# State recurrence of a Perceiver layer: B through PSUM, the product with C and half of the state sum on GpSimd

## The chip, the cores and the metric

The kernel runs on one core of a Trainium2 chip. A core has TensorE (PE in the profile, with its weight loads as PEld), VectorE (DVE), ScalarE (ACT), GpSimd (POOL) and SyncE (SP, which here only issues DMAs), each with its own queue of instructions that it takes in order; they meet through semaphores. SBUF is the working memory of 128 partitions, PSUM the memory that TensorE writes, in eight banks of 2 KB per partition. The metric is device time in microseconds (us), the median of several runs; lower is better. A line such as L893 is a line of the kernel's file.

## The reference

The kernel computes one layer over 512 latent rows of width 512: cross attention (16 heads of 64) to a context of 8192 rows, then a state-space block with its MLP, then a mixture of 16 experts. The part that matters here is the recurrence of the state-space block, over 512 steps, 1024 channels and 16 states per channel:

```python
def step(hstate, t):
    delta_t, B_t, C_t, x_t = t
    dA = jnp.exp(delta_t[..., None] * A)
    dBx = (delta_t * x_t)[..., None] * B_t[:, None, :]
    hstate = dA * hstate + dBx
    y = jnp.einsum('bdn,bn->bd', hstate, C_t)
    return (hstate, y)
```

B_t and C_t have 16 values each, the same for all channels; they come from a projection of the convolved input (`x_dbl`). The result is `y + xin * D`, multiplied by `silu(z)` and projected back.

## The kernel before

The file has two large parts. The first, up to about 1948 us of the profiled span, is the cross attention: its TensorE work is laid out by hand, and the rest of the file is ordered by the framework's scheduler, which fixes the order of each engine's queue when the kernel is built. The second part is the function `tail`, a generator, of which the first pieces (the attention's output projection for the first 256 rows, `prep(0)`, `delta(0, 0)`) run beside the attention's last unit, and the rest behind it.

In `tail` the 512 steps are two halves `s` of H = 256 steps, and the 1024 channels are eight blocks `b` of 128, which lie on the partitions. `prep(s)` normalises, projects, convolves and makes `xd`, whose rows 0 to 31 lead to delta, rows 32 to 47 are B and rows 48 to 63 are C. Both are written to DRAM (`bc_d`) and read back by `load_bc` so that every partition holds the same rows: four tiles of 4 states x 256 steps for B (k = 0) and four for C (k = 1), 512 KB each.

`delta(s, q)` makes, for a pair of blocks q, the tiles `dl` (delta), `du` (delta times the input) and `zs` (silu of z). `scan(s, b)` is the recurrence of one block, in four turns of four states each, 64 turns in all. A turn works so, with the engines in brackets:

- L886 (ScalarE), four times: dA = exp(delta x A) into columns 1 to 256 of a `dA` tile of 257 columns per state. Column 0 of dA is zero.
- L888 (ScalarE), second half only: the carried state into column 0 of the tile `hs`.
- L889 (VectorE): B x du into columns 1 to 256 of `hs`, 128x1024.
- L893 (VectorE): one scan over all 4 x 257 columns, state = dA x state + hs, in place. The zero in column 0 of dA stops one state from running into the next, and column 0 of hs is the start value.
- L895 (ScalarE), first half only: the last column into `carry`.
- L896 (VectorE): hs x C, 128x1024.
- L899 (TensorE): four matmuls with the identity add the four states into the PSUM tile `py`; in fp32 each is two records in the profile.

After four turns L900 adds D x input by one more matmul. There are three `dA` and three `hs` tiles, taken in turn. When both blocks of a pair are done, `gate` (L905 to L907, VectorE and ScalarE) multiplies `py` by `zs` and splits the product in two fp16 parts for the output projection. The pieces of `prep(1)` and, in the second half, of the first half's MLP (`ffn`) are put between the scans by the loop from L1030.

PSUM: `ps_s` (two banks), `ps_o` (one), `ps_x` (two) and `ps_j` (three) are opened for the attention and kept to the end; in `tail`, `py` takes its two buffers from `ps_s`, and accumulators of the MLP and the experts come from `ps_s`, `ps_o` and `ps_x` through `acc`.

Of the kernel before, what the change touches and what calls it, by code (L numbers as in the profile page):

```python
# [8 lines left out]
F16 = mybir.dt.float16  # L9
# [28 lines left out]
def perceiver_layer(ctx: ExitStack, tc: tile.TileContext, a: dict, out: bass.AP):  # L38
# [81 lines left out]
    ps_s = ctx.enter_context(tc.tile_pool(name="ps_s", bufs=2, space=PSUM))  # L120
    ps_o = ctx.enter_context(tc.tile_pool(name="ps_o", bufs=1, space=PSUM))
    ps_x = ctx.enter_context(tc.tile_pool(name="ps_x", bufs=2, space=PSUM))
    ps_j = ctx.enter_context(tc.tile_pool(name="ps_j", bufs=3, space=PSUM))
    L = R(late, "late", 1)
# [461 lines left out]
    for m in range(NSTEP):  # L586
        n = NLAST * NSTEP + m
        if m % 4 == 0:
            load(n // 4 + 1)
        cur = scores(u, m, loads[n // 4], sp)  # L590
        while len(pend) > 1:
            drain()
        pend.append((u, m, cur))
        if m == 0:
            tl = tail(tc, a, out, const, scr, ident, x_sb, mlp_d, oT, y_d, xd_d, (ps_s, ps_o, ps_x, ps_j))
        for _ in range(2):
            if m >= 1 and not ready:
                ready = next(tl)
# [6 lines left out]
    late.close()  # L605
    for _ in tl:
        pass


def tail(tc, a, out, const, scr, ident, x_sb, mlp_d, oT, y_d, xd_d, psums):  # L610
# [5 lines left out]
    ps_s, ps_o, ps_x, ps_j = psums  # L616
    nacc = [0]
# [9 lines left out]
    def acc(i):  # L627
        if i < 2:
            return ps_s.tile([P, DM], F32, name=f"acc{i}", tag="pss")
        nacc[0] += 1  # L630
        if nacc[0] % 3 == 0:
            return ps_o.tile([P, DM], F32, name="acc3", tag="po")
        return ps_x.tile([P, DM], F32, name="acc4", tag="px")
# [99 lines left out]
    nc.gpsimd.memset(carry, 0.0)  # L733
    bc_d = [scr.tile([32, H], F32, name=f"bc_d{s}") for s in range(2)]
# [9 lines left out]
    def prep(s):  # L744
# [86 lines left out]
        nc.scalar.copy(dtx[64:96, s], dtx[0:32, s])  # L831
        BC[s] = {}
        load_bc(s, 0, m1)
        yield

    def load_bc(s, k, pool_):
        bf = bc_d[s].rearrange("(o n) t -> o (n t)", o=1)
        for nq in range(4):
            x = pool_.tile([P, 4, H], F32, name=f"bc{k}{nq}")
            o = (k * 16 + nq * 4) * H  # L840
            nc.sync.dma_start(x.rearrange("p n t -> p (n t)"), bf[:, o : o + 4 * H].to_broadcast((P, 4 * H)))
            BC[s][k, nq] = x
# [33 lines left out]
    def scan(s, b):  # L876
        q, j = b // 2, b % 2
        if j == 0:
            dlu[s, q].append(ps_s.tile([P, 2, H], F32, name="py", tag="pss"))
        dl, du, zs, py = dlu[s, q]  # L880
        for nq in range(4):
            dA, hs = dAs[turn[0] % 3], hss[turn[0] % 3]
            turn[0] += 1
            for n in range(4):
                k = nq * 4 + n
                nc.scalar.activation(dA[:, n, 1:], dl[:, j], AF.Exp, scale=Av[:, b, k : k + 1])  # L886
            if s:
                nc.scalar.copy(hs[:, :, 0], carry[:, b, nq * 4 : nq * 4 + 4])  # L888
            nc.vector.tensor_tensor(  # L889
                hs[:, :, 1:], BC[s][0, nq], du[:, j].unsqueeze(1).to_broadcast((P, 4, H)), ALU.mult  # L890
            )
            hf = hs.rearrange("p n t -> p (n t)")
            nc.vector.tensor_tensor_scan(hf, dA.rearrange("p n t -> p (n t)"), hf, 0.0, ALU.mult, ALU.add)  # L893
            if s == 0:
                nc.scalar.copy(carry[:, b, nq * 4 : nq * 4 + 4], hs[:, :, H])  # L895
            nc.vector.tensor_mul(hs[:, :, 1:], hs[:, :, 1:], BC[s][1, nq])  # L896
            for n in range(4):
                k = nq * 4 + n
                nc.tensor.matmul(py[:, j, :], lhsT=ident, rhs=hs[:, n, 1:], start=k == 0, stop=False)  # L899
        nc.tensor.matmul(py[:, j, :], lhsT=dD[:, b], rhs=xin[s][:, b, :], start=False, stop=True)  # L900
# [113 lines left out]
    load_bc(0, 1, m3)  # L1014
    dAs = [m3.tile([P, 4, H + 1], F32, name=f"dA{i}") for i in range(3)]
    hss = [m3.tile([P, 4, H + 1], F32, name=f"hs{i}") for i in range(3)]
    for t in dAs + hss:
        nc.gpsimd.memset(t[:, :, 0:1], 0.0)
# [11 lines left out]
    for i, (s, q) in enumerate(seq):  # L1030
        scan(s, 2 * q)
        if s == 0:
            next(p1, None)
        if i:
            gate(*seq[i - 1], yTs[-1])
        if (s, q) == (1, 0):
            outproj(0, yTs[-1], h2s[0])
            ml = ffn(0, h2s[0], MLP, [acc(3), acc(3)])
            yTs.append(m3.tile([P, 2, 8, H], F16, name="yT", bufs=2))
        if ml and (s, q) != (1, 0):  # L1040
            next(ml, None)
        if i + 1 < len(seq):
            if (s, q) == (0, 3):
                for _ in p1:
                    pass
                load_bc(1, 1, m3)
            delta(*seq[i + 1])
# [9 lines left out]
    M.close()  # L1057

# [37 lines left out]
    mlp1 = ffn(1, h2s[1], MLP, [acc(0), acc(1)])  # L1096
# [6 lines left out]
    rs0 = ffn(0, xT0, RS, [acc(3), acc(3)])  # L1103
# [119 lines left out]
    def moe_down(k, gT, ws):  # L1223
        py = acc(k % 4)
# [28 lines left out]
    for _ in ffn(1, xT1, RS, [acc(3), acc(3)]):  # L1253
        pass
# [84 lines left out]
```

## Time and profile before

| | us |
|---|---|
| median of 3 runs | 2683.66 (2681.24 to 2689.78) |
| the profiled execution | 2681.84 |
| its span | 2679.8 |
| attention and lead-in, 0 to 1948 us | 1948 |
| recurrence, 1948 to 2302 us | 354 |
| MLP of the second half, experts, 2302 to 2680 us | 378 |
| VectorE busy in the recurrence | 337.4 |
| ScalarE busy there | 223.0 |
| GpSimd busy there | 4.8 |

A row of a group reads: line, engine, operation, output <- inputs, shapes, count | busy us, mean ns of one | idle time of the engine just before these instructions and what ended most of it. A row of the order of time reads: start us, duration us, engine, line, operation, and in brackets the idle time before it. Consecutive instructions of one kind may be merged into a row. Instructions of VectorE overlap by some 0.07 us at their ends, so sums of durations are larger than its busy time.

### The profile page before, as it was taken

To read this page: it belongs to the slowest core of one execution; us is meant where nothing else is said; L and a number is where in the kernel's file an instruction comes from. 1 tells how busy PE (TensorE), PEld (TensorE's weight loads), DVE (VectorE), ACT (ScalarE), POOL (GpSimd) and SP (SyncE) were. 2 spreads that over 40 slices of the span, in tenths; PEclk is the share of its full clock that TensorE was granted. 3 is DMA by queue.
4 is the path that set the end of the run, shared out by engine and by line. 5 is a ranking of instruction groups with operands and counts; after the bars stand their busy time and mean duration, and the time that the engine had idled before them with its cause. 6 is when DMAs were issued, how large, how long until landed. Compare 5 with 4: busy or idle time off the path is not lost. (4 is left out here: it accounts for less than half of the span.)

```text
span 2679.8 us, 62328 instructions
## 1 busy us (share of the span) xinstructions
PE 2429.7 (91%) x25902; PEld 1708.1 (64%) x25902; DVE 2052.3 (77%) x2355; ACT 1954.4 (73%) x3701; POOL 44.7 (2%) x58
## 2 busy tenths in 40 slices
PE   7999999999999999998999998887878777898995
PEld 4454676777666677766777767776756555665442
DVE  6786688777878877777877777886799999643785
ACT  5787787888787888867888887786857566432784
POOL 2000000000000000000000000000000000001001
PEclk8999999999999999989999999999989889999998
DMA  7873899766689966668856646666511222575896
GB/s 271 284 264 128 283 290 272 224 171 184 189 266 270 272 171 187 170 192 259 233 169 186 176 134 151 168 169 182 175 63 32 95 71 79 200 255 198 296 338 222
DMA packets 353715, 531.92 MB, mean 198 GB/s; under 512 B 25106, under 2 KB 218834, under 8 KB 353300
## 3 DMA queue, kind: packets, MB, share of 16 engines
q1 hardware_dynamic: 352148, 523.69, 64.6%
q8 instruction: 205, 3.36, 0.5%
q0 software_dynamic: 1280, 4.20, 0.5%
q14 instruction: 82, 0.67, 0.1%
HBM read 397.68 MB, written 126.94 MB: 196 GB/s over the span
## 5 line engine op out<-in xcount | busy, mean ns | idle before, releaser
L361 DVE TENSOR_TENSOR phl<-p,phl 128x1024 f16<-128x1024 f32 x512 | 625.9, 1223 | 194.1 <-ACT phl L358 156.2
L356 ACT ACTIVATE p<-pss 128x512 f32<-128x512 f32 x1024 | 601.3, 612 | 156.1 <-PE pss L349 132.4
L292 ACT ACTIVATE sf<-psx 128x512 f16<-128x512 f32 x1024 | 556.9, 620 | 83.7 <-PE psx L287 80.7
L348 PE MATMUL pss<-qhh,k 128*128 128x256 f16 x2048 | 485.5, 275 | 39.3 <-ACT phl L358 35.3
L349 PE MATMUL pss<-qlm,kb 128*128 128x256 f16 x2048 | 484.6, 275 | 0.0
L378 PE MATMUL po<-v,phl 128*128 128x65 f16 x4096 | 429.8, 195 | 25.0 <-DVE phl L361 24.8
L376 PE MATMUL po<-v,phl 128*128 128x65 f16 x4096 | 434.7, 193 | 3.2 <-DVE phl L360 1.5
L377 PE MATMUL po<-v,phl 128*128 128x64 f16 x4096 | 434.0, 193 | 0.0
L376 PEld LDWEIGHTS <-phl 128*128 128x128 f16 x4096 | 380.1, 98 | 44.5 <-issue 18.5
L378 PEld LDWEIGHTS <-phl 128*128 128x128 f16 x4096 | 379.3, 97 | 29.9 <-DVE phl L361 28.9
L377 PEld LDWEIGHTS <-phl 128*128 128x128 f16 x4096 | 379.7, 97 | 20.9 <-issue 2.0
L300 DVE TENSOR_TENSOR runm<-runm,sf 128x2048 f16<-128x2048 f16 x240 | 292.4, 1218 | 47.4 <-ACT sf L292 46.7
L358 ACT ACTIVATE phl<-pss 128x512 f16<-128x512 f32 x512 | 311.9, 609 | 0.0
L264 PE MATMUL psv<-wh_v,ctxc 128*128 128x256 f16 x1024 | 282.6, 276 | 0.0
L265 PE MATMUL psv<-wl_v,ctxc 128*128 128x256 f16 x1024 | 281.6, 275 | 0.0
L266 PE MATMUL psv<-wh_v,ctxc 128*128 128x256 f16 x1024 | 281.4, 275 | 0.0
L349 PEld LDWEIGHTS <-kb 128*128 128x128 f16 x2048 | 201.1, 98 | 94.5 <-issue 52.6
L348 PEld LDWEIGHTS <-k 128*128 128x128 f16 x2048 | 201.3, 98 | 62.4 <-issue 16.5
L287 PE MATMUL psx<-khl,qh 64*128 64x512 f16 x1024 | 210.6, 392 | 23.1 <-ACT sf L292 19.5
L360 DVE CAST phl<-p 128x1024 f16<-128x1024 f32 x256 | 176.6, 690 | 50.1 <-ACT p L356 46.3
L899 PE MATMUL py<-hs,ident 128*128 128x256 f32 x512 | 146.4, 442 | 70.8 <-DVE hs L896 70.7
L240 PE MATMUL psk<-ctxc,wh_k 128*128 128x512 f16 x512 | 197.2, 385 | 8.5 <-ACT ctxc L223 8.5
(304 smaller groups left out, 4091.3 us busy)
## 6 DMA issues: line engine op xcount, KB each, us to landing
v<-v_d SPq DMA_DIRECT2D x128, 520.0 KB, 4.7
k<-k_d SPq DMA_DIRECT2D x256, 256.0 KB, 4.6
ctxc<-ctx_d SPq DMA_DIRECT2D x96, 512.0 KB, 6.1
wef<-in_gu_dram SPq DMA_DIRECT2D x72, 512.0 KB, 6.2
v_d<-vs SPq DMA_DIRECT2D x128, 260.0 KB, 3.4
k_d<-khl SPq DMA_DIRECT2D x128, 256.0 KB, 3.0
kb<-k_d SPq DMA_DIRECT2D x128, 256.0 KB, 5.2
wpm<-w_d SPq DMA_DIRECT2D x48, 512.0 KB, 4.6
```

What stands on the lines that cost most here:

```text
L264: nc.tensor.matmul(ps[:, t, :], lhsT=ct[i // 2][:, 0, i % 2, sl], rhs=wh[:, i, :], start=i == 0, stop=False)
L265: nc.tensor.matmul(ps[:, t, :], lhsT=ct[i // 2][:, 0, i % 2, sl], rhs=wl[:, i, :], start=False, stop=False)
L292: nc.scalar.activation(dst, ps, AF.Copy, scale=1.0 / (8.0 * WS))
L300: nc.vector.tensor_tensor(r, r, sf, ALU.max)
L348: nc.tensor.matmul(ps[:, hh], lhsT=k[:, hh, sl], rhs=qhh[:, hh, qs], start=True, stop=False)
L349: nc.tensor.matmul(ps[:, hh], lhsT=b[:, hh, sl], rhs=qlm[:, hh, qs], start=False, stop=True)
L356: nc.scalar.activation(p32[:, i], pss[i], AF.Exp, scale=sc)
L358: nc.scalar.activation(ph[:, i], pss[i], AF.Exp, scale=sc)
L361: nc.vector.tensor_tensor(pl, p32, ph, ALU.subtract)
L376: nc.tensor.matmul(o, lhsT=ph[:, i, hh, qs], rhs=vh1, start=first, stop=False, **kw)
L377: nc.tensor.matmul(o[:, 0:64], lhsT=ph[:, i, hh, qs], rhs=vl, start=False, stop=False, **kw)
L378: nc.tensor.matmul(o, lhsT=pl[:, i, hh, qs], rhs=vh1, start=False, stop=last, **kw)
```

## The change

B no longer comes as broadcast tiles. In `prep`, B times 16 is split into three fp16 parts, and three small DMAs put them into rows 0 to 2 of a tile `bhl` whose other rows are zero. A matmul with a weight tile that holds 1/16 everywhere then adds the three rows and gives every partition the sum, 2 states x 256 steps at a time, in a PSUM tile `pb` of two buffers. VectorE multiplies `pb` by `du` in place in PSUM, and scans with dA from SBUF and `pb` from PSUM into `hs`; a turn has two such halves. The tiles dA and hs have 256 columns per state instead of 257: dA's first column is zero, and in the second half the carried state times its decay (`dc`) is added into the first column of `pb` before the scan. The carry is now copied by VectorE.

The product with C runs on GpSimd. In every second turn GpSimd also adds the turn's last two states to its first two, so that TensorE sums two tiles instead of four there. The `gate` of a pair of blocks is called inside the next pair's first scan, after its first turn's product, because `py` has one buffer now. The attention's PSUM pools are closed before the recurrence; it opens a pool of its own (`py` one bank, `pb` two, accumulators two), and a pool of five accumulators follows behind it. The C tiles are loaded by `load_c`, as those of k = 1 were.

```diff
+    bhl = [m1.tile([P, 16 * H], F16, name=f"bhl{s}") for s in range(2)]
+    for t in bhl:
+        nc.gpsimd.memset(t, 0.0)
+    sixteenth = m1.tile([P, P], F16, name="sixteenth")
+    nc.gpsimd.memset(sixteenth, 1.0 / WS)
...
+        bs = m2.tile([64, 3, H], F16, name="bs", tag="w2k", bufs=5)
+        br = m2.tile([64, H], F32, name="br", tag="w2k", bufs=5)
+        rows = slice(32, 48)
+        nc.scalar.activation(bs[rows, 0], xd[rows], AF.Copy, scale=WS)
+        nc.vector.scalar_tensor_tensor(br[rows], xd[rows], WS, bs[rows, 0], ALU.mult, ALU.subtract)
+        nc.scalar.copy(bs[rows, 1], br[rows])
+        nc.vector.tensor_tensor(bs[rows, 2], br[rows], bs[rows, 1], ALU.subtract)
+        for x in range(3):
+            nc.sync.dma_start(bhl[s][x : x + 1, :].rearrange("o (n t) -> o n t", t=H), bs[rows, x])
         BC[s] = {}
-        load_bc(s, 0, m1)
...
+        if s:
+            dc = m2.tile([P, 16], F32, name="dc", bufs=2)
+            nc.scalar.activation(dc, Av[:, b, :], AF.Exp, scale=dl[:, j, 0:1])
+            nc.vector.tensor_mul(dc, dc, carry[:, b, :])
...
-                nc.scalar.activation(dA[:, n, 1:], dl[:, j], AF.Exp, scale=Av[:, b, k : k + 1])
-            if s:
-                nc.scalar.copy(hs[:, :, 0], carry[:, b, nq * 4 : nq * 4 + 4])
-            nc.vector.tensor_tensor(
-                hs[:, :, 1:], BC[s][0, nq], du[:, j].unsqueeze(1).to_broadcast((P, 4, H)), ALU.mult
-            )
-            hf = hs.rearrange("p n t -> p (n t)")
-            nc.vector.tensor_tensor_scan(hf, dA.rearrange("p n t -> p (n t)"), hf, 0.0, ALU.mult, ALU.add)
+                nc.scalar.activation(dA[:, n, 1:], dl[:, j, 1:], AF.Exp, scale=Av[:, b, k : k + 1])
+            for n2 in range(2):
+                k, ns = nq * 4 + 2 * n2, slice(2 * n2, 2 * n2 + 2)
+                pb = accs[-1].tile([P, 2, H], F32, name="pb", tag="pb", bufs=2)
+                nc.tensor.matmul(
+                    pb.rearrange("p n t -> p (n t)"), lhsT=sixteenth, rhs=bhl[s][:, k * H : (k + 2) * H],
+                    start=True, stop=True,
+                )
+                nc.vector.tensor_tensor(pb, pb, du[:, j].unsqueeze(1).to_broadcast((P, 2, H)), ALU.mult)
+                if s:
+                    nc.vector.tensor_tensor(pb[:, :, 0], pb[:, :, 0], dc[:, k : k + 2], ALU.add)
+                nc.vector.tensor_tensor_scan(
+                    hs[:, ns].rearrange("p n t -> p (n t)"), dA[:, ns].rearrange("p n t -> p (n t)"),
+                    pb.rearrange("p n t -> p (n t)"), 0.0, ALU.mult, ALU.add,
+                )
             if s == 0:
-                nc.scalar.copy(carry[:, b, nq * 4 : nq * 4 + 4], hs[:, :, H])
-            nc.vector.tensor_mul(hs[:, :, 1:], hs[:, :, 1:], BC[s][1, nq])
-            for n in range(4):
-                k = nq * 4 + n
-                nc.tensor.matmul(py[:, j, :], lhsT=ident, rhs=hs[:, n, 1:], start=k == 0, stop=False)
+                nc.vector.tensor_copy(carry[:, b, nq * 4 : nq * 4 + 4], hs[:, :, H - 1])
+            nc.gpsimd.tensor_tensor(hs, hs, BC[s][nq], ALU.mult)
+            two = nq % 2
+            if two:
+                nc.gpsimd.tensor_tensor(hs[:, 0:2], hs[:, 0:2], hs[:, 2:4], ALU.add)
+            if before:
+                before()
+                before = None
+            if j == 0 and nq == 0:
+                dlu[s, q].append(accs[-1].tile([P, 2, H], F32, name="py", tag="py", bufs=1))
+            py = dlu[s, q][3]
+            for n in range(2 if two else 4):
+                nc.tensor.matmul(py[:, j, :], lhsT=ident, rhs=hs[:, n, :], start=nq == 0 and n == 0, stop=False)
...
+    pb_s = ExitStack()
+    accs.append(pb_s.enter_context(tc.tile_pool(name="ps_b", bufs=2, space=PSUM)))
+    load_c(0, m3)
...
-        scan(s, 2 * q)
+        scan(s, 2 * q, (lambda: gate(*seq[i - 1], yTs[-1])) if i else None)
         if s == 0:
             next(p1, None)
-        if i:
-            gate(*seq[i - 1], yTs[-1])
...
     M.close()
+    pb_s.close()
+    accs.append(es.enter_context(tc.tile_pool(name="ps_a", bufs=5, space=PSUM)))
```

## The prediction

> **What bounds the kernel now.** I read three views, in this order: busy time by stretch, the groups of instructions in the stretch that the change touches, and the order of time inside it. The state recurrence (`scan`) runs from 1948 us to 2302 us of the span.
>
> ```profile
> core 0: us, PE busy (x) PEld busy (x) DVE busy (x) ACT busy (x) POOL busy (x), PEclk, DMA share, GB/s
> 0.00:1948.00 1948.00, 1832.86 (x22375) 1311.72 (x22376) 1493.85 (x1755) 1536.86 (x2961) 22.99 (x37) 0.98 0.72 210
> 1948.00:2302.00 354.00, 273.79 (x1413) 206.73 (x1412) 337.41 (x301) 223.04 (x497) 4.78 (x5) 0.91 0.21 67
> ```
>
> In this stretch VectorE (DVE) works 337.4 of 354 us, ScalarE 223, the DMA engines a fifth, GpSimd (POOL) 5. VectorE sets the pace here. The groups of the stretch say with what:
>
> ```profile
> L893 DVE TENSOR_TENSOR_SCAN hs<-dA,hs 128x1028 f32<-128x1028 f32 x64 | 145.1, 2287 | 2.8 <-ACT dA L886 2.4
> L896 DVE TENSOR_TENSOR hs<-hs,bc 128x1024 f32<-128x1024 f32 x64 | 76.7, 1212 | 0.8 <-ACT carry L895 0.8
> L889 DVE TENSOR_TENSOR hs<-bc,du 128x1024 f32<-128x1024 f32 x64 | 76.0, 1213 | 0.9 <-PE py L899 0.7
> L905 DVE TENSOR_TENSOR y<-py,zs 128x512 f32<-128x512 f32 x8 | 5.4, 677 | 2.9 <-PE py L900 2.9
> L864 DVE TENSOR_TENSOR du<-dl,xin 128x512 f32<-128x512 f32 x7 | 4.8, 684 | 0.0
> L899 PE MATMUL py<-hs,ident 128*128 128x256 f32 x512 | 146.4, 442 | 70.8 <-DVE hs L896 70.7
> ```
>
> There are 64 turns (2 halves x 8 blocks x 4 groups of 4 states); each costs VectorE a product with B (L889), a scan (L893) and a product with C (L896). Almost no idle time stands before them. TensorE (PE) waits 70.7 us for L896. The order of time shows the pitch:
>
> ```profile
> 2040.06 1.20 DVE L889 TENSOR_TENSOR hs<-bc,du 128x1024 f32<-128x1024 f32 x1
> 2041.18 1.22 DVE L896 TENSOR_TENSOR hs<-hs,bc 128x1024 f32<-128x1024 f32 x1
> 2042.32 2.29 DVE L893 TENSOR_TENSOR_SCAN hs<-dA,hs 128x1028 f32<-128x1028 f32 x1
> 2042.45 2.00 PE L899 MATMUL py<-hs,ident 128*128 128x256 f32 x8 [0.17 <-DVE hs L896]
> 2044.53 1.20 DVE L889 TENSOR_TENSOR hs<-bc,du 128x1024 f32<-128x1024 f32 x1
> ```
>
> Start to start, the products take 1.12 and 1.14 us, the scan 2.21: a turn is 4.47 us of VectorE, 64 turns 286 us. The other 51 of its 337 us are `delta`, `gate`, the second `prep`, norms and splits. The four sums over states of a turn are eight matmul records in about 1.8 us of issue.
>
> **The change, VectorE's demand.** The product with C leaves VectorE: -1.13 us a turn. The product with B and the scan become two halves of 512. From the rows, one element of a product costs (1.13 - 0.06)/1024 and of a scan (2.21 - 0.07)/1028 us, so halves have a pitch of 0.60 and 1.14 us; a turn becomes 2 x 0.60 + 2 x 1.14 = 3.48 us. That is -0.99 x 64 = -63 us. Added: 32 copies of the carry, 64 additions of two elements, 8 products of 16, small splits: about 106 small instructions; such ones (L920, 0.13 us long) start 0.06 to 0.08 us before the next one, so +7 us. VectorE's demand falls from 337 to 281 us, 4.4 a turn.
>
> [...] The row of L905 reads PSUM and takes 677 ns, L864 reads SBUF alone and takes 684. [...]
>
> **GpSimd's price.** It gets 64 products of 1024 and 32 additions of 512. The nearest row is four additions of 512:
>
> ```profile
> L182 POOL TENSOR_TENSOR x_sb<-x_sb,bo_bc x4: 1441/1732/2250, 24.8 to 29.6; 128x512 f32<-128x512 f32 x4
> 24.83 7.04 POOL L182 TENSOR_TENSOR x_sb<-x_sb,bo_bc 128x512 f32<-128x512 f32 x4 [11.73 <-DMA bo_bc<-in_bo_dram]
> ```
>
> Doubled, a product is 2.9 us by the fastest and 3.6 by the mean. [...] During those four, VectorE ran two-input SBUF work (L224, L80). [...]
>
> **What takes the place of the removed work.** In the built order of the changed kernel, TensorE's queue holds the broadcasts of B for turn t+1 mostly behind the sums of turn t-1, and these wait for GpSimd. So a chain closes over two turns: scan t-1 ends, GpSimd multiplies (and adds, in every second turn), TensorE sums, broadcasts, VectorE does turn t+1. Even: hop 0.05 + 2.32 + 0.05 + sums 1.76 + broadcast and hop 0.45 (a 128x512 matmul is 0.38) + 3.56 = 8.2 us. Odd: 0.05 + 2.32 + 1.24 + 0.05 + 0.88 + 0.45 + 3.56 = 8.55. With the small additions of the second half that is 4.23 a turn, 271 us. On top:
> - Other matmuls (z, FFN, convolution) stand between those sums and the next broadcast: about 67 us counted over all turns by the pitches 0.109 (256 columns) and 0.215 (512 columns), of which one parity's chain sees half, 33, and 36 at the clock of 0.91.
> - In seven turns the broadcast stands behind the sums of the turn right before: about 1.7 us beyond what other VectorE work covers, +12. In ten it stands a turn further ahead: -7.
> - Of VectorE's other 51 us most fits into the waits (the chain leaves about 1.3 us a turn); a quarter I count on the chain, +10.
>
> Sum 322 us for the 64 turns.
>
> **Start and end.** Before, the recurrence starts while TensorE is busy with the projection of the attention output:
>
> ```profile
> 1947.22 3.48 DVE L889 TENSOR_TENSOR hs<-bc,du 128x1024 f32<-128x1024 f32 x3
> 1950.81 2.30 DVE L893 TENSOR_TENSOR_SCAN hs<-dA,hs 128x1028 f32<-128x1028 f32 x1
> 1957.95 0.38 PE L688 MATMUL pwo<-wpm,oT 128*128 128x512 f16 x1
> 1958.16 1.89 PE L899 MATMUL py<-hs,ident 128*128 128x256 f32 x8
> ```
>
> After, the first broadcasts stand behind all 48 matmuls of that projection, so the first product starts at about 1958.7, some 11 us later. At the end GpSimd has memsets and the affine select (4.34 us by its row) ahead of its last product, so the last gate comes about 7.7 us after the last scan instead of 5.4 (2295.0 to 2300.4). 1958.7 + 322 + 7.7 = 2288 against 2300: -12 us.
>
> **At nothing.** ScalarE loses 64 small copies of 0.19 us and gains splits; it isn't full. SP loses eight broadcast loads of B (512 KB, 6.2 us to landing) and gains six small loads that fill the three rows of B; the first three are issued in the last attention unit, with tens of us of cover, the second three before the first half's last block is scanned. Uncovered, a chain of loads would cost about 6 us once. Clearing those rows takes GpSimd 2 x 3.8 us (0.95 per 1024, L710) while it is idle. The later stages keep their instructions; their PSUM pools rotate over five buffers. I allow 3 us either way.
>
> Profiled execution 2681.8 (span 2679.8 and 2 us around it) - 12 = 2670; the median of the runs is 1.8 above that execution, so 2672.
>
> **The rivals.**
> - *VectorE stays the bound* (0.20): its idle moments and the matmuls' coincide, the chain is hidden. 281 us of work + its 17 of idle now = 298, + 10 at the start + 2 at the end against 354: -44, 2640. For it: the chain alone is 4.23 a turn against 4.4. Against: the queues are in order and the broadcasts have two PSUM buffers.
> - *GpSimd is slow* (0.27): at 2.9 and 1.45 us the chain grows by 0.58 or 0.79 per two turns, half of that per turn, +22 us; at the mean row +45. So 2694 to 2717, I take 2700. This is the one on the other side. It decides from 0.2 us more a turn (+12 us), a product of about 2.65 us. For it: the only row. Against: what VectorE ran beside that row.
> - *Nothing measurable* (0.17): start delay, in-order matmuls and PSUM's fixed cost eat the rest: 2682.
>
> **How the numbers follow.** Likeliest case 0.36, 2672, its own range 2655 to 2688. Measurement tells about 0.3% (8 us) from no change. Faster: 0.31 of the likeliest, 0.20, and 0.02 of the third, 0.53. Same: 0.04 of the likeliest and 0.13, 0.17. Slower: 0.27 and the rest, 0.30. The range leaves out the tenth beyond a hidden chain and that beyond the mean row: 2640 to 2704.
>
> **What would show it.** Right: the groups of the halves at 0.68 and 1.21 us with no product with C on VectorE; GpSimd's products near 2.3 us; VectorE idle some 40 us or more in the stage, ended by TensorE's broadcasts; the first half-product near 1958. Wrong: products of GpSimd at 2.9 us or more, or stretched by VectorE; halves over 0.75 or 1.3 us (PSUM's price); VectorE still over 95% busy (then faster than I say); or sums that wait on GpSimd with long rows of other matmuls behind them, on average over 5 us a turn.

## The result, and the profile after

The changed kernel takes 2756.50 us (2744.96 to 2763.28) against 2686.72 us (2681.24 to 2690.23) for the kernel before on the same chip: 1.0257 times as long, with a 95% interval of 1.0213 to 1.0301. I had forecast 2672 us, faster, with 2640 to 2704 as the range. The prediction was wrong, in sign and in size. The profiled execution took 2751.74 us, with a span of 2750.0 us against 2679.8 before. Of these +70.2 us:

| stretch of the span | before, us | after, us | difference | forecast |
|---|---|---|---|---|
| last split of the attention's output starts | 1946.8 | 1959.5 | +12.7 | 0 |
| from there to the first product with B | 0.4 | 10.5 | +10.1 | +11.5 |
| from there to the start of the last gate | 353.2 | 403.5 | +50.3 | -23.5 |
| from there to the end | 379.4 | 376.5 | -2.9 | 0 |

Busy time by stretch, changed kernel (columns: the stretch, its length, busy time and instructions of the engines, granted clock of TensorE, DMA share, GB/s):

```profile
core 0: us, PE busy (x) PEld busy (x) DVE busy (x) ACT busy (x) POOL busy (x), PEclk, DMA share, GB/s
0.00:1970.00 1970.00, 1851.23 (x22420) 1319.66 (x22421) 1500.30 (x1761) 1545.91 (x2979) 30.05 (x37) 0.97 0.70 207
1970.00:2374.00 404.00, 287.95 (x1385) 193.57 (x1385) 319.44 (x470) 217.00 (x426) 194.93 (x101) 0.90 0.17 54
```

No engine is full in the recurrence. VectorE was busy 337.4 of 354 us before; it is busy 319.4 of 404 us now, and idle for 84.6. I had forecast 281 us of work in a stage of about 330 us, so some 49 us of idle time. VectorE has 38 us more work than that, and 36 us more idle time. These two numbers are what has to be explained. (The windows and groups here and below are of one profiled execution of each kernel.)

The groups of that stretch, changed kernel. Three lines are pieces that the change left alone (L869 and L872 in `delta`, L935 in `gate`):

```profile
L916 POOL TENSOR_TENSOR hs<-hs,bc 128x1024 f32<-128x1024 f32 x64 | 151.6, 2369 | 217.2 <-DVE carry L915 99.7 <-DVE hs L910 82.5 <-PE pxz L679 12.4
L910 DVE TENSOR_TENSOR_SCAN hs<-dA,pb 128x512 f32<-128x512 f32 x128 | 150.3, 1206 | 1.0 <-DVE pb L909 0.4
L927 PE MATMUL py<-hs,ident 128*128 128x256 f32 x384 | 118.6, 452 | 92.0 <-POOL hs L919 54.0 <-POOL hs L916 37.8
L907 DVE TENSOR_TENSOR pb<-pb,du 128x512 f32<-128x512 f32 x128 | 84.9, 690 | 43.5 <-PE pb L903 43.4
L919 POOL TENSOR_TENSOR hs<-hs 128x512 f32<-128x512 f32 x32 | 42.7, 1334 | 2.5
L869 DVE SCALAR_TENSOR_TENSOR ex<-u,ex 128x512 f32<-128x512 f32 x7 | 10.5, 1494 | 0.6 <-ACT u L867 0.6
L935 DVE TENSOR_TENSOR yT<-y,yT 128x512 f16<-128x512 f32 x7 | 9.2, 1310 | 0.6 <-ACT yT L934 0.6
L872 DVE TENSOR_TENSOR dl<-rl,lgu 128x512 f32<-128x512 f32 x7 | 8.0, 1148 | 0.0
L642 DVE TENSOR_TENSOR r<-r,nw_a 128x2 f32<-128x2 f32 x1 | 2.2, 2194 | 0.0
```

Read the means first. The halves (L907 at 690 ns, L910 at 1206) and GpSimd (2369 and 1334) are what I had forecast. The same three pieces took 684, 680 and 681 ns before and now take 1494, 1310 and 1148; L642, on two elements per partition, took 0.15 us and now takes 2.19. The same four in the kernel before:

```profile
L859 DVE SCALAR_TENSOR_TENSOR ex<-u,ex 128x512 f32<-128x512 f32 x7 | 4.8, 684 | 2.1 <-ACT u L857 2.0
L907 DVE TENSOR_TENSOR yT<-y,yT 128x512 f16<-128x512 f32 x7 | 4.8, 680 | 0.0
L862 DVE TENSOR_TENSOR dl<-rl,lgu 128x512 f32<-128x512 f32 x7 | 4.8, 681 | 0.1
L645 DVE TENSOR_TENSOR r<-r,nw_a 128x2 f32<-128x2 f32 x1 | 0.1, 146 | 0.0
```

Then the last column of the changed kernel's groups: TensorE's sums wait 92.0 us for GpSimd.

The waits of VectorE in the stretch, changed kernel (who waited <- for whom: us in total, times, the longest):

```profile
DVE pb L907 <- PE pb L903: 43.4, 33, 5.8
DVE g L972 <- PE pu L679: 16.4, 6, 6.1
DVE y L933 <- PE py L928: 9.1, 4, 5.6
DVE xs L780 <- ACT xs L778: 7.3, 2, 3.7
```

The broadcasts end 43.4 us of idle time, as forecast. Another 33 us are ended by other work, most of it TensorE's, for which VectorE waited far less before: the MLP's `pu` (it is called FFN in the file), the last sum ahead of a gate, a split of `prep`.

The order of time says when this happens. In a stretch with no long turn the turns start 3.62, 3.88 and 4.43 us apart (over all 64 turns the scans of one turn end 6.26 us behind those of the turn before on average, 5.54 in the median):

```profile
2256.12 1.27 DVE L907 TENSOR_TENSOR pb<-pb,du 128x512 f32<-128x512 f32 x2
2259.74 1.27 DVE L907 TENSOR_TENSOR pb<-pb,du 128x512 f32<-128x512 f32 x2
2263.62 1.35 DVE L907 TENSOR_TENSOR pb<-pb,du 128x512 f32<-128x512 f32 x2 [0.17 <-PE pb L903]
2268.05 0.70 DVE L907 TENSOR_TENSOR pb<-pb,du 128x512 f32<-128x512 f32 x1 [0.65 <-PE pb L903]
```

But seven times more than 10 us lie between the end of one turn's scans and the end of the next turn's; these seven stretches take 93 us and hold 47.7 us of VectorE's idle time. One of them:

```profile
2093.75 2.35 POOL L916 TENSOR_TENSOR hs<-hs,bc 128x1024 f32<-128x1024 f32 x1 [2.78 <-DVE carry L915]
2096.18 1.26 POOL L919 TENSOR_TENSOR hs<-hs 128x512 f32<-128x512 f32 x1
...
2097.49 2.08 PE L927 MATMUL py<-hs,ident 128*128 128x256 f32 x4 [2.32 <-POOL hs L919]
2099.36 1.06 PE L928 MATMUL py<-xin,dD 128*128 128x256 f32 x2
2100.22 0.63 PE L860 MATMUL pd<-dtx,dtw 128*128 128x256 f16 x2
...
2103.27 0.27 PE L679 MATMUL pz<-hT,wpm 128*128 128x256 f16 x1
2103.38 0.59 PE L903 MATMUL pb<-bhl,sixteenth 128*128 128x512 f16 x2
2103.80 1.30 DVE L907 TENSOR_TENSOR pb<-pb,du 128x512 f32<-128x512 f32 x2 [5.81 <-PE pb L903]
```

TensorE waits for GpSimd's addition, does its sums, then the next block's delta and 24 matmuls of z (2100.64 to 2103.38), and only then the broadcast that VectorE has been waiting for.

### The profile page after: what moved, and what is told of

Same layout as the page of the kernel before. It is cut to its first block, busy times and chain, and to the rows that moved or that the text cites. A ratio compares the mean times of both kernels' runs of the same rounds, so it can differ in the third digit from the quotient of the medians.

```text
span 2750.0 us, 62689 instructions
## 1 busy us (share of the span) xinstructions
PE 2461.3 (90%) x25902; PEld 1701.9 (62%) x25902; DVE 2039.2 (74%) x2527; ACT 1957.2 (71%) x3649; POOL 241.2 (9%) x154
## 5 line engine op out<-in xcount | busy, mean ns | idle before, releaser
L927 PE MATMUL py<-hs,ident 128*128 128x256 f32 x384 | 118.6, 452 | 92.0 <-POOL hs L919 54.0
```

## The experiments

Two explanations were set against each other. *Queue* (Q in some of the expectations): the sums over states wait for GpSimd in TensorE's queue, and everything behind them waits too, so where a row stands in that queue decides. *Contention* (L): GpSimd and VectorE hold each other up at SBUF, wherever anything stands. A third, P, put the loss on the broadcasts through two PSUM buffers alone; the first three runs below lie under its limits of 2720, 2720 and 2735 us. Where no other kernel is named, a diff is against the changed kernel. A ratio is to the kernel before on the same chip, whose median there was 2686.7 to 2689.7 us, so that medians of different rows can be compared to about 3 us. All the runs, with the stretch from the first product with B to the last gate's end as "stage":

| kernel | median us | ratio to before (95%) | stage | VectorE busy in it |
|---|---|---|---|---|
| before | 2686.72 | | 353.9 | 338.2 |
| changed | 2756.50 | 1.0257 (1.0213 to 1.0301) | 404.2 | 319.6 |
| no product with C | 2689.83 | 1.0014 (0.9997 to 1.0030) | 344.1 | 289.3 |
| sums read another tile | 2681.19 | 0.9977 (0.9960 to 0.9994) | 332.0 | 315.1 |
| product with C on VectorE | 2715.91 | 1.0113 (1.0051 to 1.0174) | 372.3 | 355.5 |
| before, product with C on GpSimd | 2756.50 | 1.0264 (1.0198 to 1.0330) | 417.7 | 364.2 |
| sums one turn later | 2739.30 | 1.0195 (1.0162 to 1.0227) | 386.2 | 317.2 |
| sums two turns later | 2716.39 | 1.0096 (1.0065 to 1.0126) | 364.2 | 318.2 |
| projection moved | 2749.13 | 1.0224 (1.0196 to 1.0252) | 408.2 | 314.1 |
| no addition on GpSimd | 2758.02 | 1.0246 (1.0213 to 1.0279) | 404.4 | 309.0 |
| two turns + projection | 2705.20 | 1.0066 (1.0044 to 1.0087) | 369.1 | 319.4 |
| ... + fourth buffer | 2707.39 | 1.0062 (1.0040 to 1.0084) | 367.8 | 312.9 |
| ... + three turns | 2693.62 | 1.0021 (1.0012 to 1.0031) | 355.0 | 320.5 |
| ... + sources in PSUM | 2687.35 | 0.9999 (0.9987 to 1.0011) | 347.2 | 309.0 |
| changed, no clearing | 2751.41 | 1.0238 (1.0220 to 1.0256) | 408.5 | 319.3 |
| sources in PSUM, no clearing | 2693.04 | 1.0016 (1.0001 to 1.0030) | 354.9 | 307.7 |
| sources in PSUM, clearing on VectorE | 2675.42 | 0.9946 (0.9930 to 0.9962) | 344.4 | 309.2 |

### The parts of the change, one by one

No product with C, and no addition on GpSimd:

```diff
-            nc.gpsimd.tensor_tensor(hs, hs, BC[s][nq], ALU.mult)
-            two = nq % 2
-            if two:
-                nc.gpsimd.tensor_tensor(hs[:, 0:2], hs[:, 0:2], hs[:, 2:4], ALU.add)
+            two = 0
```

> The changed kernel without the product with C and without the addition of states on GpSimd: TensorE sums the raw states, four per turn (the product with C is left out of the computation). Theory Q (the latency of GpSimd sits in a chain through TensorE's in-order queue to the next broadcast): the chain is gone, VectorE is the bound with about 281 us of work, some 10 us of start delay stay: 2645 to 2670 us. Rival P (the broadcasts of B through two PSUM buffers and TensorE's order are what costs): stays above 2720.

Measured: 2689.83 us, between the two ranges on record. Neither text had seen what TensorE does without GpSimd's addition:

```profile
1962.40:2306.50 344.10, 299.78 (x1526) 199.46 (x1527) 289.32 (x470) 220.45 (x429) 0.73 (x5) 0.98 0.20 64
```

VectorE is busy 289.3 us, 8 more than the 281 of the forecast and 30.3 less than in the changed kernel, although its instructions are the same. TensorE, which sums four tiles in every turn here, is busy 299.8 of 344.1, and VectorE still idles 54.8 us:

```profile
PE py L924 <- DVE hs L910: 38.1, 59, 2.7
DVE pb L907 <- PE pb L903: 36.8, 35, 2.5
```

The sums now wait for the scan, and broadcasts still stand behind them. So even with GpSimd idle, this arrangement with four sums in every turn is no faster than the kernel before (2689.83 us; the profiled execution, 2682.08, is the fastest of its ten), and GpSimd's latency alone doesn't account for the 84.6 us of idle time in the changed kernel.

The sums read dA instead of the products, so that they no longer wait for GpSimd, nor for the scan, as dA is ready before it; GpSimd does all its work, and only the reuse of `hs` waits for it. The sum over states is left out (it adds up other numbers):

```diff
-                nc.tensor.matmul(py[:, j, :], lhsT=ident, rhs=hs[:, n, :], start=nq == 0 and n == 0, stop=False)
+                nc.tensor.matmul(py[:, j, :], lhsT=ident, rhs=dA[:, n, :], start=nq == 0 and n == 0, stop=False)
```

> The changed kernel with all of GpSimd's work, but TensorE sums the dA tiles instead of the products (the sum over states is left out of the computation), so no sum waits for GpSimd; only the reuse of the hs tiles does. Theory Q: the latency is off the chain and only the stretching of VectorE's instructions beside GpSimd stays (about 31 us by the profile of the changed kernel): 2675 to 2705 us. [...] Rival P: 2720 or more.

Measured: 2681.19 us, in the queue's range; at 2735 us or more the contention would have been the main cost. The stage falls by 72 us with all of GpSimd's work still there:

```profile
1968.30:2300.30 332.00, 262.70 (x1370) 185.04 (x1369) 315.12 (x467) 214.03 (x425) 195.13 (x100) 0.92 0.19 63
```

```profile
L927 PE MATMUL py<-dA,ident 128*128 128x256 f32 x383 | 101.1, 402 | 2.1 <-ACT dA L899 1.4 <-DVE y L933 0.3 <-DVE carry L915 0.3
```

The sums wait 2.1 us in all. VectorE's busy time stays high (315.1) and its idle time falls from 84.6 to 16.9 us. So the sums' wait in the queue makes the idle time, and something else makes the work longer. How much of that wait is GpSimd's and how much the scan's, this run doesn't tell; in the run before it, with the scan's alone and 64 more sums, VectorE idled 54.8 us.

The product with C back on VectorE, four sums, B still by broadcast:

```diff
-            nc.gpsimd.tensor_tensor(hs, hs, BC[s][nq], ALU.mult)
-            two = nq % 2
-            if two:
-                nc.gpsimd.tensor_tensor(hs[:, 0:2], hs[:, 0:2], hs[:, 2:4], ALU.add)
+            nc.vector.tensor_tensor(hs, hs, BC[s][nq], ALU.mult)
+            two = 0
```

> The changed kernel with the product with C back on VectorE and four sums per turn on TensorE; B still comes through PSUM. Q: VectorE's work is about 281 + 72 = 353 us, 16 more than before, and the start delay of 10 us stays: 2705 to 2720 us. L: the same, as GpSimd is idle. P: 2735 or more.

Measured: 2715.91 us, as expected. B by TensorE costs 1.1% by itself: the late start, and small instructions and splits that bring VectorE to 355.5 us. Moving the product with C, and half of the state sum, to GpSimd then adds 40 us instead of taking time away. With GpSimd idle, the split of the gate takes 683 ns here.

The kernel before, with the product with C on GpSimd and nothing else changed (B in SBUF, no broadcast by TensorE):

```diff
-            nc.vector.tensor_mul(hs[:, :, 1:], hs[:, :, 1:], BC[s][1, nq])
+            nc.gpsimd.tensor_tensor(hs[:, :, 1:], hs[:, :, 1:], BC[s][1, nq], ALU.mult)
```

> The kernel before with only the product with C moved to GpSimd; B stays in SBUF, the scan and the product with B have two SBUF inputs. L: both are stretched by GpSimd's 150 us of products, or stretch them: 2740 us or more. Q without any contention: VectorE loses 73 us of work, no broadcast waits for the sums: 2625 to 2650 us.

Measured: 2756.50 us, not 2625 to 2650. Here there is no broadcast to be late. VectorE is busy 364.2 us although it lost a product of 76.7 us, so the rest of its work grew by some 100 us, more than the move saves; its idle time grew by another 38 us. The groups of its recurrence:

```profile
L896 POOL TENSOR_TENSOR hs<-hs,bc 128x1024 f32<-128x1024 f32 x64 | 189.8, 2974 | 223.9 <-ACT carry L895 115.8 <-DVE hs L893 93.3 <-DVE id L1090 3.6
L893 DVE TENSOR_TENSOR_SCAN hs<-dA,hs 128x1028 f32<-128x1028 f32 x64 | 177.4, 2791 | 4.9 <-ACT dA L886 4.0
L889 DVE TENSOR_TENSOR hs<-bc,du 128x1024 f32<-128x1024 f32 x64 | 108.0, 1701 | 18.6 <-PE py L899 17.7 <-issue 0.3
```

The scan takes 2791 ns (2287 before), the product with B 1701 (1213), and GpSimd's product 2974 instead of 2369. All read two sources from SBUF. That the halves, with B in PSUM, kept their price in the changed kernel fits this.

### The place of the sums

The same instructions, with the sums of a turn emitted two turns later, the gate one turn later (core of the edit; `sums` holds the matmuls of L927 and L928):

```diff
+    def flush(keep=0):
+        while len(late_py) > keep:
+            late_py.pop(0)()
...
-            if before:
+            flush(1)
+            if before and nq == 1:
                 before()
                 before = None
-            py = dlu[s, q][3]
-            for n in range(2 if two else 4):
-                nc.tensor.matmul(py[:, j, :], lhsT=ident, rhs=hs[:, n, :], start=nq == 0 and n == 0, stop=False)
+            late_py.append(lambda hs=hs, nq=nq, two=two: sums(s, b, nq, two, hs))
```

> Same instructions as the changed kernel; only the place of the sums over states in TensorE's queue moves: the sums of a turn are emitted two turns later (and the gate one turn later), so that the rows of other matmuls which stood between the sums of turn t-1 and the broadcast of turn t+1 (67 us over all turns by their pitches) now stand ahead of the sums, and a sum meets a product of GpSimd that is long done. Queue theory (sums that wait for GpSimd hold up the broadcasts behind them): the eight long turns shrink from 10-14 us to 6-8, the stage from 403 to 345-365 us, 2700-2725 us in all. Contention theory (stretched VectorE and GpSimd instructions): the order matters little, at least 2740 us.

One turn later, the gate where it was:

```diff
-            flush(1)
-            if before and nq == 1:
+            flush()
+            if before:
```

> Same instructions; the sums of a turn are emitted one turn later. That removes the seven places where a broadcast stands behind the sums of the turn right before it, and takes the rows between sums and the broadcast after next from 67 to 46 us. Queue theory: 12 us for the tight places and half of 21 us for the rows, so 2730-2745 us. Contention theory: 2750-2760 us.

Measured: 2716.39 and 2739.30 us, 40 and 17 us less than the changed kernel, both in the queue's ranges and outside the other's. VectorE's busy time does not move (318.2 and 317.2); its idle time falls from 84.6 to 46.0 and 69.0. The order alone is worth these 40 us. What goes are the long turns: with the sums two turns later the median from turn to turn is 5.57 us, as before (5.54), but only one is over 10 us instead of seven.

The second projection of the attention output after the first four turns:

```diff
-    for _ in wo_proj(1):
-        pass
     xin[1] = const.tile([P, 2, 8, H], F32, name="xin1", tag="big16")[:, 0]
...
         scan(s, 2 * q, (lambda: gate(*seq[i - 1], yTs[-1])) if i else None)
+        if not i:
+            for _ in wo_proj(1):
+                pass
```

> The second projection of the attention output is emitted after the first four turns instead of before them, so that the first two broadcasts stand ahead of its 48 matmuls. If the late start costs what its 10 us say, about 2746 us. If the matmuls only move in between the first turns, where sums wait for GpSimd, and are paid there, 2752-2758 us.

Measured: 2749.13 us, 7 less, between the two; the intervals of the two kernels overlap. In the profile the recurrence starts 10 us earlier and takes 4 us longer.

No addition on GpSimd, four sums in every turn:

```diff
-            two = nq % 2
-            if two:
-                nc.gpsimd.tensor_tensor(hs[:, 0:2], hs[:, 0:2], hs[:, 2:4], ALU.add)
+            two = 0
```

> GpSimd keeps the product with C but adds nothing; TensorE sums four tiles in every turn, as before the change. GpSimd loses 32 additions of 1.33 us, TensorE gains 64 matmuls of 0.44 us in 32 turns. Queue theory: per two turns the chain loses 1.33 and gains 0.88 us, so 0 to 10 us faster, 2746-2757 us. If GpSimd's time itself is the bound, up to 43 us faster, 2714-2730. If TensorE's time is the bound, up to 28 us slower, 2765-2785.

Measured: 2758.02 us, no different from the changed kernel. Taking 42.7 us of work from GpSimd gains nothing, so GpSimd's total is not the bound. VectorE's busy time falls by 10.6 us, as less of GpSimd's work runs beside it, but its idle time rises by as much, to 95.4 us, while TensorE has 64 sums more. So less work for VectorE isn't yet time gained while the sums still stand where they do.

Both reorderings; then also a fourth buffer for `hs` (the diagonal of D is made in every block to make room); then that buffer used to emit the sums three turns later:

```diff
-            dA, hs = dAs[turn[0] % 3], hss[turn[0] % 3]
+            dA, hs = dAs[turn[0] % 3], hss[turn[0] % 4]
...
-            flush(1)
-            if before and nq == 1:
+            flush(2)
+            if before and nq == 2:
```

> Both reorderings together: the sums two turns later and the second projection of the attention output after the first four turns. If the start and the long turns are separate losses, the gains of 40 and 7 us add up: 2707-2711 us. If the projection's matmuls are then paid in the recurrence instead, 2714-2720 us.

> As the run before it, with a fourth buffer for the products of the scan (the diagonal of D is made in every block instead of once, to make room). Queue theory: a scan of turn t+3 no longer waits for the sums of turn t, which still wait for GpSimd; VectorE's idle 46 us fall to 25-35, 2690-2702 us. If what is left is contention (VectorE's 318 us busy instead of the 281 forecast), no change, 2705-2711 us.

> The fourth buffer used to emit the sums three turns later (the gate two turns later), so that every sum has a product of GpSimd that is at least a turn old. Queue theory: sums no longer wait, the stage comes to the 332 us of the run in which the sums read another tile, 2672-2690 us. If each turn is then held by the contention or by TensorE's own order, 2700-2710 us.

Measured: 2705.20, 2707.39 and 2693.62 us. The two gains add up (51 us, where 40 and 7 make 47). The fourth buffer alone does nothing; my expectation of 2690 to 2702 was wrong, since what waited was the sums, not the reuse of `hs`. With the sums three turns later the stage is 355.0 us, not the 332 that I had named, and the time lies between the two ranges on record: VectorE is busy 320.5 and idle 34.5 us. Its work is now nine tenths of the stage, and with it the contention counts, though the sums still wait 42.8 us for GpSimd.

### The contention

On the last kernel, one of the two sources of three kinds of VectorE instructions goes from SBUF to PSUM, by writing the instruction before it in place:

```diff
-        rl = w2("rl")
+        rl = pd
...
-        y = m2.tile([P, 2, H], F32, name="y", tag="w2k", bufs=5)
-        nc.vector.tensor_mul(y, py, zs)
+        nc.vector.tensor_mul(py, py, zs)
+        y = py
...
-            nc.vector.scalar_tensor_tensor(g, pu, IW, g, ALU.mult, ALU.mult)
+            nc.vector.scalar_tensor_tensor(pu, pu, IW, g, ALU.mult, ALU.mult)
+            g = pu
```

> As the run with the sums three turns later, with one of two sources of three kinds of VectorE instructions moved from SBUF to PSUM by writing the instruction before it in place: the remainder of the gate's split reads y in PSUM, the remainder of the FFN's split reads g in PSUM, the sum that gives delta reads the relu in PSUM. Nothing else changes. Contention theory (VectorE is stretched beside GpSimd only where it reads two sources from SBUF): the three rows fall from 1336, 1126 and 949 ns to about 690, together 8 us of VectorE, which is the bound there with 320 of 355 us, so 2684-2690 us. If the stretch has another cause, such as VectorE waiting for its turn whatever it reads, the rows keep their means and the time stays at 2691-2696 us.

Measured: 2687.35 us. The three rows in the kernel with sums three turns later, then with one source in PSUM:

```profile
L948 DVE TENSOR_TENSOR yT<-y,yT 128x512 f16<-128x512 f32 x7 | 9.4, 1336 | 0.0
L988 DVE TENSOR_TENSOR gg<-g,gg 128x512 f16<-128x512 f32 x7 | 8.2, 1166 | 2.1 <-ACT gg L987 2.1
L872 DVE TENSOR_TENSOR dl<-rl,lgu 128x512 f32<-128x512 f32 x7 | 6.6, 949 | 0.1
```

```profile
L948 DVE TENSOR_TENSOR yT<-py,yT 128x512 f16<-128x512 f32 x7 | 4.7, 672 | 0.0
L989 DVE TENSOR_TENSOR gg<-pu,gg 128x512 f16<-128x512 f32 x7 | 4.8, 685 | 2.4 <-ACT gg L988 2.4
L872 DVE TENSOR_TENSOR dl<-pd,lgu 128x512 f32<-128x512 f32 x7 | 4.7, 677 | 0.0
```

All three are back at the price they had beside an idle GpSimd (680, 683 and 681 ns in the kernel before). VectorE's busy time falls by 11.5 us, the stage by 7.8, the median by 6.3. For these three it is the second SBUF source on which the stretch beside GpSimd hangs.

### The part ahead of the recurrence

The attention ended 12.7 us later with the same instructions. In the changed kernel's order of time, GpSimd's clearing of a tile of B's rows, and VectorE at that moment:

```profile
1836.52 3.51 POOL L733 MEMSET bhl<- 128x4096 f16 x1 [216.16 <-DVE phl L362]
```

```profile
1836.52 4.06 DVE L361 CAST phl<-p 128x1024 f16<-128x1024 f32 x1
```

The cast's median is 0.69 us over 256 of them, of which the one shown is the longest: it starts with the clearing, and its 4.06 us are 3.4 more than the median, against 3.51 of the clearing. All twelve kernels that clear on GpSimd have this cast, and in their profiles the unit of the attention that it falls in takes 59.7 to 60.0 us, from the fourteenth of its 16 splits to the fifteenth, against 55.7 in the kernel before. The next two kernels leave the clearing out and let the broadcast contract over the three filled rows, on the changed kernel and on the one with sources in PSUM:

```diff
-    for t in bhl:
-        nc.gpsimd.memset(t, 0.0)
...
-                    pb.rearrange("p n t -> p (n t)"), lhsT=sixteenth, rhs=bhl[s][:, k * H : (k + 2) * H],
+                    pb.rearrange("p n t -> p (n t)"), lhsT=sixteenth[0:3, :], rhs=bhl[s][0:3, k * H : (k + 2) * H],
```

> The changed kernel without the two clearings of the rows of B on GpSimd (3.51 us each, in the last two attention units): the broadcast contracts over the three filled rows alone instead of 128, so the other rows need not be zero. In the trace one clearing stands beside a VectorE cast of 4.06 us, whose median is 0.69. If the clearing holds the cast, no cast is over 1 us, the last split of the attention output ends 3 to 7 us earlier (1953-1957 us instead of 1959.5), and the time falls by as much, 2749-2753 us. If the cast was late for another reason, no change, 2755-2758 us.

> The run with one source in PSUM, and without the clearings. If the clearing held VectorE for 3 to 7 us on the path, 2680-2684 us, faster than the kernel before. If not, 2686-2689 us.

Measured: 2751.41 and 2693.04 us. The longest cast is 0.81 us in both, and that unit is back at 55.8 us. The attention ends 5 and 2 us earlier (1955 and 1958). On the changed kernel the median falls by 5 us, as expected, though the intervals overlap; on the other it rises by 6, against my expectation. Its recurrence took 354.9 us instead of 347.2. The stage with 128 rows, then with three:

```profile
1959.40:2306.60 347.20, 275.71 (x1434) 192.16 (x1433) 309.03 (x474) 222.91 (x453) 193.36 (x101) 0.94 0.21 66
```

```profile
1956.90:2311.80 354.90, 300.64 (x1435) 186.09 (x1434) 307.69 (x474) 222.64 (x453) 193.85 (x101) 0.91 0.20 64
```

TensorE's granted clock is 0.91 instead of 0.94, and it is busy 25 us longer with as many matmuls. On the changed kernel the clock falls from 0.90 to 0.86 with the three rows. By the ratio of the two clocks, 276 us would become some 285 (an estimate), so the clock accounts for less than half of the 25 us. The order of time shows another part; a broadcast and what follows it, with 128 rows and with three:

```profile
2051.84 0.38 PE L920 MATMUL pb<-bhl,sixteenth 128*128 128x512 f16 x1
2052.06 2.75 PE L800 MATMUL pc<-xp,dg 128*128 128x256 f32 x12
```

```profile
2052.33 0.39 PE L918 MATMUL pb<-bhl,sixteenth 3*128 3x512 f16 x1
2052.64 2.86 PE L798 MATMUL pc<-xp,dg 128*128 128x256 f32 x12
```

The next matmul starts 0.31 us after the broadcast of three rows, 0.22 after that of 128 (medians of 95 such places: 0.314 and 0.215). A broadcast of three rows also starts later behind a sum (0.312 against 0.216 us, medians of 34 and 29). So TensorE loses about 0.1 us at each change between products of 3 and of 128 rows. To separate the clearing from the shape, the last kernel keeps the 128 rows and clears on VectorE:

```diff
-        nc.gpsimd.memset(t, 0.0)
+        nc.vector.memset(t, 0.0)
```

> The run with one source in PSUM, with the two clearings of the rows of B on VectorE instead of GpSimd; the broadcasts contract over 128 rows again. It separates the clearing from the shape of the broadcast: in the run that took both away the attention part ended 2 us earlier, but the recurrence took 354.9 us instead of 347.2 and TensorE's granted clock there was 0.91 instead of 0.94. If the three-row broadcasts lowered the clock, the clock is back at 0.94, the recurrence at about 347 us, and the time 2682-2686 us, 2 to 5 below the 2687.4 of the run with one source in PSUM. If the longer recurrence had nothing to do with the shape, the clock stays near 0.91 and the time is 2689-2694 us.

Measured: 2675.42 us, 0.9946 (0.9930 to 0.9962) of the kernel before: faster than both, and 7 us below the expected range.

```profile
1951.00:2295.40 344.40, 271.94 (x1435) 189.54 (x1433) 309.20 (x474) 222.98 (x454) 193.48 (x101) 0.95 0.21 66
```

The clock is back at 0.95, the stage is 344.4 us, and the next matmul follows after 0.215 us again. So the lower clock and the longer recurrence came with the narrow broadcast; how much of the longer recurrence each of its two effects makes is not separated. VectorE clears a tile in 1.77 us. The attention ended at 1952 us here, 8 earlier than with the clearing on GpSimd; the unit with the cast accounts for 3 of that (56.8 us), the rest is open. That this kernel ends 3 us from the 2672 of the forecast doesn't make the forecast's sum right: the recurrence takes 344.4 us here, where 329.7 to the last gate's start were forecast, and it starts 8 us sooner than the forecast had it (1951.0 against 1958.7).

## Why the prediction was wrong

The forecast for the profiled execution was 2670 us, and it took 2751.74. Of these 82 us, 74 arose between the first product and the last gate (38 of VectorE's work, 36 of its waits) and 13 ahead of it; the start and the end give back 4.

**VectorE bounds the kernel before.** Nothing in the runs speaks against it: with B by TensorE and the product with C left on VectorE, it was busy 355.5 of 372.3 us.

**The halves.** Right. Pitches of 0.60 and 1.14 us were forecast; two products and two scans of an undisturbed turn take 1.18 and 2.23 us, 0.59 and 1.12 each, and all of them together 223.9 us against the 223 of the forecast (each counted to its end or to the start of VectorE's next instruction, as here below). The forecast had nothing in them for PSUM, by the rows of L905 and L864 (677 and 684 ns), and that held: L907 takes 690 ns, reading and writing PSUM, against the 684 of an SBUF instruction. No run shows the price of PSUM that stands beside the limits of 0.75 and 1.3 us and in the rival "nothing measurable".

**GpSimd's price.** Right in size: 2369 and 1334 ns, 194.3 us in all, against the 2.32 and 1.24 us in the forecast's sum. No run ahead of the result shows those two terms; the one row there was, four additions of 128x512, took 1441 to 2250 ns. Nor did a run show then that VectorE's work beside that row made it long; the later run with B in SBUF has products of 2974 ns. The product stayed under the 2.65 us from which the rival "GpSimd is slow" would have decided. That rival had the right sign with the wrong mechanism. (Its upper end, by the mean row, comes to about +50 us by the prediction's own numbers, not +45; nothing hangs on it.)

**VectorE's demand: the first step that failed.** GpSimd is now busy 194.9 of the 404 us, and much of VectorE's work outside the halves reads two SBUF sources (L869, L935 and L872 took 1494, 1310 and 1148 ns instead of 684, 680 and 681). I carried that rest over at its old price, 51 us, and added 7 for small instructions. This rest took 95.7 us instead of 58. Of the 37.7 us, 30.8 are gone with GpSimd idle (64.9 us in the kernel without the product with C). Some 6 are the small new instructions, which take 13 us there and not 7: the 64 additions stand 0.11 us from what follows, the 32 copies 0.13, where I had read 0.06 to 0.08 off one row. One source from SBUF was no safeguard for all of it: L751, a TENSOR_SCALAR of 128x2 with one, took 2268 ns beside a product of GpSimd and 168 with GpSimd idle. What the 31 us cost in time on the changed kernel, no run shows by itself; on the kernel with the sums three turns later, 11.5 us less of VectorE's work made the stage 7.8 us shorter.

**The chain through TensorE's queue: the second step that failed.** The mechanism is as described: the chain over two turns, the broadcasts as the end of VectorE's waits, 43.4 us of them. In a stretch with no long turn a turn takes 3.98 us on average (3.62 to 4.43), under its 4.23. What failed is the term "Of VectorE's other 51 us most fits into the waits", of which only a quarter stood on the chain. The waits are not spread at 0.8 or 1.3 us a turn. They come where a block ends and delta, z, a gate or a piece of the FFN stand behind sums that wait for GpSimd: seven turns take 93 us, the other 56 counted 5.4 us each, where I had 5.0 on average over all. VectorE's own other work comes at the same places, and it waits there for TensorE, too: 16.4 us for `pu`, 9.1 for `py`, which my chain did not have at all. Work and waits therefore stand one behind the other. The stage is 319.4 + 84.6 us, where I had 281 + 49. My last sign of being wrong, sums that wait for GpSimd with long rows behind them and over 5 us a turn, is what came: 6.26 us. That emitting the sums two turns later gains 40 us, as much as my terms for the rows behind the sums and the tight places (36 + 12 - 7 = 41), does not show these terms right: with them in the sum, the stage was still forecast 74 us too short.

**Start and end.** The first product stood behind all 48 matmuls of the projection, 10.1 us later against 11.5 forecast. The last gate starts 5.5 us after the last scan, not 7.7.

**At nothing: the third step that failed.** "Clearing those rows takes GpSimd 2 x 3.8 us while it is idle" priced the clearing by GpSimd's own time. It holds VectorE: one cast for 3.4 us, and the unit that it falls in is 4.2 us longer. The rest of the 12.7 us is not settled: 4.0 us of it are lost between 1216 and 1341 us, where the code is the same, and the profiles of kernels that share that code end this part up to 8 us apart. The twelve kernels with the clearing end the attention anywhere from 1951.9 to 1963.0 us. The later stages' 3 us held (-2.9).

**Nothing measurable** (2682) was not it, though its mechanism, gains eaten by other terms, is close to what the kernel without the product with C does.

## What to carry to other kernels

Work moved to another engine is priced by who stands in a queue behind its result: put the consumer as many turns later as the buffers allow before the move is judged (here 63 us, of which the projection's place is 7 to 11). While GpSimd runs, look at the price of every VectorE instruction on the path, the small and old ones too (here one went from 0.15 to 2.19 us); moving one of two SBUF sources to PSUM brought three of them back to theirs (1336, 1166 and 949 ns to 672, 685 and 677). Don't take work of GpSimd, even a clearing, for free because GpSimd is idle (a cast of 0.69 us took 4.06 beside one of 3.51). Sum demand and waits of a stage where they fall in time, not as an average per turn.

## What the runs showed that I had not expected

- A broadcast by a matmul over 3 rows instead of 128 is no shorter (400 against 388 ns), the matmul behind it starts 0.1 us later, and TensorE's granted clock in the stage fell from 0.94 to 0.91, and from 0.90 to 0.86 in the other pair; the fp32 sums beside it went from 452 to 484 ns there.
- A VectorE cast of 0.69 us took 4.06 us beside a GpSimd clearing of 3.51 us, which reads nothing.
- VectorE instructions on two elements per partition (L642, L751) took 2.2 and 2.3 us instead of 0.15 and 0.17. Each started 0.1 to 0.2 us after a GpSimd product of 2.3 us and ended with it, so these two lost nearly the whole product. The 64 additions on two elements in PSUM (L909) kept 160 ns.
- With the same instructions, the order of the sums alone moved the time from 2756.5 to 2716.4 us.
